# A decoder layer on one core: softmax on ScalarE, one memory region for the feed-forward block, and operand sums moved into the first unit

## The chip, the cores and the metric

The kernel runs on one core of a Trainium2 chip. The metric is the device time of one execution in microseconds (us). A core has five engines that run side by side, each with a queue of its own: TensorE (PE, whose weight loads are shown apart as PEld), VectorE (DVE), ScalarE (ACT), GpSimd (POOL) and SyncE (SP), whose queue issues the DMA transfers here. SBUF is the working memory, PSUM the memory that PE writes to.

## What is computed

One pre-norm decoder layer over x of shape (4, 2048, 512): a recurrence along the first axis (four steps), cross attention to a context of 77 keys for each of the four rows with 16 heads of 32, and a feed-forward block whose hidden size is 2048 and whose weights are a dense matrix times a butterfly, on the way up and on the way down. All of it is fp32. Cut to what matters:

```python
def _L0_xattn_ref(query, context, Wq, Wk, Wv, Wo):
    Q = (query @ Wq.T).reshape(B, T_q, N_HEADS, D_HEAD)
    K = (context @ Wk.T).reshape(B, T_c, N_HEADS, D_HEAD)
    V = (context @ Wv.T).reshape(B, T_c, N_HEADS, D_HEAD)
    scale = jnp.sqrt(jnp.asarray(D_HEAD, dtype=query.dtype))
    scores = jnp.einsum('bqhd,bkhd->bhqk', Q, K) / scale
    attn = jax.nn.softmax(scores, axis=-1)
    out = jnp.einsum('bhqk,bkhd->bqhd', attn, V).reshape(B, T_q, D)
    return out @ Wo.T

def _L0_ffn_ref(x, W_exp, b_exp, up_weights, up_bias, down_weights, W_con, b_con, down_bias):
    h = jnp.einsum('bsd,dh->bsh', x, W_exp) + b_exp
    h = butterfly(h, up_weights, D_HIDDEN)
    h = jax.nn.gelu(h + up_bias, approximate=False)
    h = butterfly(h, down_weights, D_HIDDEN)
    y = jnp.einsum('bsh,hd->bsd', h, W_con) + b_con
    return y + down_bias

x = x + _L0_attn_ref(_layernorm(x, axis=-1), ...)
x = x + _L0_xattn_ref(_layernorm(x, axis=-1), ctx_1024, ...)
x = x + _L0_ffn_ref(_layernorm(x, axis=-1), ...)
```

## The kernel before

**Preparation.** `_prepare` (L321) multiplies each butterfly into its dense matrix on the chip. The products pass through two large tiles: `wup` (4 x 2048 floats a partition) and `wdn` (16 x 512). At its end, the loop at L464 makes the 16 blocks of the down matrix with PE (L466) and evicts them into `wdn`. The down product isn't multiplied plainly, but by a scheme of 26 products of blocks, whose right operands are blocks of this matrix (`PLAIN`) and sums of them (`RIGHT`, 18 sums in two lots of nine). After every fourth block the sums of one quarter (j = 0 to 3) are made at once, half of them on DVE and half on POOL (L483, with one L480 among them), in a stretch of `wup` that is free by then, and stored in `dn26` in HBM (L484). The plain blocks are stored at the end (L488). Each sum has 256 elements a partition.

**Units.** The 2048 columns are worked in 16 units of 128. A unit has a front (`front`, L609: norm, recurrence, norm, query projection, attention, output projection, norm) and a feed-forward part (`feed_forward`, L738). The front of unit u + 1 is a generator, of which pieces are taken in between the feed-forward's matmuls of unit u (`step`, L750): PE has the work of both in its queue. The front of unit 0 runs inside the preparation, and the feed-forward of unit 15 has no front beside it. The projections and the up product run as seven block products for eight (`seven`, L593, and `up_head`, `up_mid`, `up_tail`), so operand sums on DVE and POOL stand ahead of them: `t2`, `t3` at L634 to L636, `sw` at L703 to L706, and `combine` (L727), which makes t1, t2 on DVE (L732, L734) and t3, n4 on POOL (L733, L735).

**Attention.** For each row t the four groups of four heads have one score matmul each (L662), into one of the two banks of PSUM tag "f", which all of the front shares. DVE takes the maximum of each head (L666) and subtracts it (L667), ACT makes the exponentials of the four heads in one instruction (L668). After four groups DVE sums (L670) and inverts (L671), and POOL multiplies (L672). After the scores of row t + 1 PE transposes the probabilities of row t (L684); the copies to SBUF alternate between DVE (L689) and ACT (L687), and the products with the values follow (L694).

**Output projection.** The first of the seven products goes to three quarters of xt. `spread` (L714) copies it from PSUM by ACT (L715) and adds it three times on POOL (L717); the other products are added to xt by DVE (L712).

**Feed-forward.** Eight steps p, each with weights of 896 KB (`w_up`, L779) and three PSUM tags a, b, c of two banks each; four Gelus a step on ACT (L772), and DVE's sums in between. Their outputs go into four `quarter` tiles. In the second half and through the down product POOL makes the left operands (L821, `made`) in the order of `_down_plan`. The down product is 26 products (L857), whose operands are loaded in turn into three weight buffers, and whose results DVE adds to xt (L872, L874). POOL adds the last bias to xt in eight pieces (L832).

**Memory.** The preparation's tiles lie in a pool (`prep`) that is closed after it. The feed-forward's pools (`xlast`, `acts`, `wts0` to `wts2`, `ffn`) are opened then and take over its memory, so that their first tiles wait for the last use of what lay there. `xlast` holds the x of every third unit.

**Order.** Inside the preparation PE, SP and POOL take their instructions in the order in which the program writes them; later the scheduler of the language orders each engine's queue, by the program's order and what it reckons to be ready. SP's queue holds all DMA issues in one line.

## Time and profile before

The median of three runs is 2778.08 us (2777.43 to 2786.68). The profiled execution took 2783.32 us, of which 2781.5 are the span from its first to its last instruction.

| group of instructions | count | busy us | mean ns |
|---|---|---|---|
| ACT exp, L668 (four heads, 308 elements) | 256 | 109.1 | 457 |
| ACT table loads, L668 and L772 | 75 + 75 | 192.4 | 1283 |
| ACT Gelu from SBUF, L772 | 384 | 194.8 | 508 |
| ACT Gelu from PSUM, L772 | 128 | 60.0 | 469 |
| DVE maximum, L666 | 256 | 119.9 | 473 |
| DVE subtraction, L667 | 256 | 113.8 | 470 |
| DVE sum, L670 (1232 elements) | 64 | 91.1 | 1424 |
| POOL multiplication, L672 (1232 elements) | 64 | 143.9 | 2248 |
| POOL addition in spread, L717 (512 elements) | 48 | 59.5 | 1269 |
| DVE addition of a projection, L712 (512 elements) | 96 | 66.0 | 687 |

Busy time is what the engine spent on instructions of the group; where neighbours overlap, the mean times the count is more than the busy time. In the lines of a timeline the columns are start, busy time, engine, line and operation, output and input, shape and count; in brackets stands how long the engine idled before and what ended that. In the lines of waits they are who waited, for whom, the sum in us, how often, and the longest.

### The profile page before, as it was taken

What the parts mean: (1) busy time and instruction counts of PE and PEld (TensorE: products, weight loads), DVE (VectorE), ACT (ScalarE), POOL (GpSimd) and SP (SyncE); (2) the same over time, 40 slices, a digit from 0 to 9 for tenths busy, and PEclk for the clock granted to TensorE, in tenths of its full rate; (3) what the DMA queues carried; (4) which work ended last, traced back from release to release, by engine and by line L of the source; (5) the groups of instructions that cost most, each with busy time, mean ns of one, the idle gap of its engine ahead of it and who ended that gap; (6) DMA issues with size and microseconds to landing.
All of it is one profiled execution on the core that took longest, in us unless ns stands there. A gap on an engine that the chain in (4) does not pass through costs nothing.

```text
span 2781.5 us, 37646 instructions
## 1 busy us (share of the span) xinstructions
PE 2564.9 (92%) x14280; PEld 2153.5 (77%) x14280; DVE 1610.1 (58%) x3653; ACT 840.9 (30%) x1484; POOL 1110.5 (40%) x957
## 2 busy tenths in 40 slices
PE   8886999898999989899998999999999998989999
PEld 5765778787878878787887878778787877878788
DVE  6666555555665655566555556655565565556542
ACT  2331414134241412424141341514234150422411
POOL 4543441626244261614416252351624335162434
PEclk9997999999999999999999999999999999999999
DMA  5736253443535344353534435253353534334356
GB/s 168 242 110 228 106 184 115 152 177 122 212 118 189 111 163 166 121 212 117 181 119 152 178 122 211 103 178 136 131 193 113 203 125 159 143 137 180 119 186 238
DMA packets 137894, 439.54 MB, mean 158 GB/s; under 512 B 20209, under 2 KB 46961, under 8 KB 134897
## 3 DMA queue, kind: packets, MB, share of 16 engines
q1 hardware_dynamic: 137714, 437.13, 43.9%
q8 instruction: 114, 1.87, 0.3%
q14 instruction: 66, 0.54, 0.1%
HBM read 398.27 MB, written 38.81 MB: 157 GB/s over the span
## 4 chain that ended last, share of the span: by engine, by line
PE 54%; DVE 19%; POOL 17%; DMA 4%; issue 3%; ACT 2%; SPq 1%; POOLq 0%; DVEq 0%; ACTq 0%
PE ps_b L767 9%; PE ps_c L767 6%; PE ps_q L604 6%; PE ps_a L767 5%; PE ps_w L604 4%; POOL pr L672 4%; POOL x L821 4%; POOL tb L821 4%; PE ps_b L857 4%; PE ps_s L619 3%; POOL q L821 3%; PE ps_pt L684 3%; DMA w_up<-up 3%; PE ps_sc L662 3%; DVE st L525 3%
## 5 line engine op out<-in xcount | busy, mean ns | idle before, releaser
L767 PE MATMUL ps_b<-tb,w_up 128*128 128x256 f32 x1512 | 392.0, 380 | 0.0
L672 POOL TENSOR_TENSOR pr<-pr,sm 128x1232 f32<-128x1232 f32 x64 | 143.9, 2248 | 440.1 <-DVE sm L671 436.7
L767 PEld LDWEIGHTS ps_b<-tb,w_up 128*128 128x128 f32 x1512 | 281.5, 190 | 39.9 <-issue 2.8
L772 ACT ACTIVATE q<-q,hbias 128x256 f32<-128x256 f32 x384 | 194.8, 508 | 334.7 <-DVE q L808 207.2
L767 PE MATMUL ps_a<-xnt,w_up 128*128 128x256 f32 x1008 | 262.8, 381 | 7.6 <-DMA w_up<-up 7.1
L561 ACT COPY xnt<-ps_t 128x512 f32<-128x512 f32 x128 | 73.7, 588 | 566.5 <-PE ps_t L560 566.5
L684 PE MATMUL ps_pt<-ident,pr 128*77 128x128 f32 x1024 | 166.1, 304 | 83.6 <-POOL pr L672 81.0
L821 POOL TENSOR_TENSOR x<-q 128x512 f32<-128x512 f32 x32 | 40.6, 1268 | 502.9 <-ACT q L772 502.9
L684 PEld LDWEIGHTS ps_pt<-ident,pr 128*77 128x77 f32 x1024 | 132.4, 164 | 130.4 <-POOL pr L672 98.5
L767 PEld LDWEIGHTS ps_a<-xnt,w_up 128*128 128x128 f32 x1008 | 188.0, 190 | 38.9 <-DMA w_up<-up 13.5
L712 DVE TENSOR_TENSOR xt<-ps_w,xt 128x512 f32<-128x512 f32 x96 | 66.0, 687 | 208.4 <-POOL xt L717 118.3
L689 DVE COPY pt<-ps_pt 77x512 f32<-77x512 f32 x128 | 87.5, 684 | 144.1 <-PE ps_pt L684 143.9
L662 PE MATMUL ps_sc<-kbd,qt 128*128 128x308 f32 x512 | 161.9, 427 | 7.4 <-DVE pr L667 6.7
L604 PE MATMUL ps_q<-xnt,wq 128*128 128x256 f32 x640 | 151.1, 379 | 0.0
L821 POOL TENSOR_TENSOR q<-q,x 128x512 f32<-128x512 f32 x48 | 61.1, 1273 | 225.1 <-PE ps_a L857 223.9
L604 PE MATMUL ps_w<-wo,sw 128*128 128x256 f32 x512 | 124.3, 386 | 28.1 <-DVE xt L712 23.9
L857 PE MATMUL ps_b<-w_dn,q 128*128 128x256 f32 x640 | 148.5, 379 | 0.0
L666 DVE TENSOR_REDUCE mx<-ps_sc 128x4 f32<-128x308 f32 x256 | 119.9, 473 | 42.2 <-PE ps_sc L662 37.0
L668 ACT ACTIVATE pr<-pr 128x308 f32<-128x308 f32 x256 | 109.1, 457 | 108.1 <-DVE pr L667 106.6
L687 ACT COPY pt<-ps_pt 77x512 f32<-77x512 f32 x128 | 74.2, 580 | 215.9 <-PE ps_pt L684 215.7
L821 POOL TENSOR_TENSOR x<-q,q 128x512 f32<-128x512 f32 x80 | 114.2, 1428 | 61.9 <-ACT q L772 55.6
L857 PE MATMUL ps_b<-w_dn,x 128*128 128x256 f32 x512 | 135.9, 384 | 0.0
(236 smaller groups left out, 5616.4 us busy)
## 6 DMA issues: line engine op xcount, KB each, us to landing
w_dn<-dn SPq DMA_DIRECT2D x416, 512.0 KB, 4.2
w_up<-up SPq DMA_DIRECT2D x126, 896.0 KB, 4.5
wq<-wq SPq DMA_DIRECT2D x16, 1792.0 KB, 8.4
xt<-in_x SPq DMA_DIRECT2D x16, 1024.0 KB, 5.4
out<-xt SPq DMA_DIRECT2D x48, 256.0 KB, 2.4
dn<-wup SPq DMA_DIRECT2D x8, 1152.0 KB, 5.2
wdn<-in_wexp_t SPq DMA_DIRECT2D x4, 1024.0 KB, 10.3
wdn<-in_wcon SPq DMA_DIRECT2D x4, 1024.0 KB, 4.8
```

Of the source, the lines that this page charges most:

```text
L525: keep(nc.vector.bn_stats(st[:, t, :], xt[:, t, :]))
L604: nc.tensor.matmul(tiles[key][:, r, :], lhsT=lhs(i, r, k), rhs=rhs(i, r, k), start=key == i and r == 0 and k == 0, stop=k == 1, skip_group ...
L662: nc.tensor.matmul(ps[:, 0 : 4 * NK], lhsT=qt[:, g, t, :], rhs=kbd[:, t, g, :], start=True, stop=True)
L666: nc.vector.tensor_reduce(mx, sc, AX.X, ALU.max)
L668: nc.scalar.activation(pg, pg, AF.Exp, scale=1.0 / math.sqrt(DH))
L672: nc.gpsimd.tensor_tensor(pr, pr, sm.unsqueeze(2).to_broadcast([P, NH, NK]), ALU.mult)
L684: nc.tensor.transpose(pt_ps[0:NK, j, :], pr[:, 4 * g + j, :], ident)
L689: nc.vector.tensor_copy(pt, pt_ps[0:NK])
L767: nc.tensor.matmul(ps, lhsT=w[:, c, :], rhs=rhs[i - 1][:, c], start=first and c == 0, stop=c == 1, skip_group_check=True)
L772: nc.scalar.activation(out, x, AF.Gelu, bias=hbias[:, b : b + 1])
L821: nc.gpsimd.tensor_tensor(place(p), place(x), place(y), ALU.add if op == "+" else ALU.subtract)
L857: nc.tensor.matmul(ps, lhsT=left[:, j, :], rhs=pair[:, n, j, :], start=first and j == 0, stop=j == NB // 4 - 1, skip_group_check=True)
```

## The change

It has four parts.

- **Softmax.** The keys are scaled by -1/sqrt(32) when they are laid out, so that a score comes out negated. DVE takes the minimum of each head; ACT makes the exponential of each head by itself, straight from PSUM, with the minimum as bias and a scale of -1, and delivers the sum with it (`accum_out`). The subtraction and the sum on DVE go. DVE instead of POOL multiplies by the inverse.
- **Spread.** DVE adds the first product of the output projection to three quarters of xt straight from PSUM; ACT's copy and POOL's additions go.
- **One region.** `arena` is one tile of 20480 floats a partition that lives through the whole kernel. The preparation's `wup`, `wdn` and `low` and, after it, xlast, the sums' places, tb, p1, u2, u3, two of the three weight buffers and the four quarters are slices of it. The weights of the up product's third and fourth step are loaded ahead of the first unit.
- **Operand sums.** Those of quarter 0 are made in the preparation, on POOL alone; those of quarters 1 to 3 in the first three steps of unit 0, seven on DVE and eleven on POOL each. The blocks of `wdn` are laid in the order in which they are made, and all eight plain blocks of a quarter are stored with its sums. A sign is turned in e and in the right operand 4. In unit 0 the last bias is added in two pieces.

```diff
-FIRST = 0, NB // 2, NB // 4, 3 * NB // 4
+ORDER = [k + j for j in range(4) for k in (0, NB // 2, NB // 4, 3 * NB // 4)]
...
-PLAIN = ("b01", "b10", "b11", "b20", "b30", "b31")
+PLAIN = tuple(f"b{k}{n}" for k in range(4) for n in range(2))
+SLOW = "12", "9", "7", "18", "15", "16", "20", "17", "10", "19", "22"
...
+def _right_sums(nc, j, wdn, rings, dn26, alone):
+
+    made = {f"b{k}{d}": wdn[:, 4 * j + k, d * (D // 2) : (d + 1) * (D // 2)] for k in range(4) for d in range(2)}
+    for lot, ring in zip(RIGHT, rings):
+        w = ring.rearrange("p (s d) -> p s d", s=len(lot))
+        for i, (name, x, op, y) in enumerate(lot):
+            made[name] = w[:, i, :]
+            x, y, op = made[x], made[y], ALU.add if op == "+" else ALU.subtract
+            if alone or name in SLOW:
+                nc.gpsimd.tensor_tensor(made[name], x, y, op)
+            else:
+                nc.vector.tensor_tensor(made[name], x, y, op)
+        first = SLOT[lot[0][0]]
+        nc.sync.dma_start(out=dn26[first : first + len(lot), :, j, :].rearrange("s p d -> p s d"), in_=w)
+    nc.sync.dma_start(out=dn26[2 * len(RIGHT[0]) : 2 * len(RIGHT[0]) + 8, :, j, :].rearrange("s p d -> p s d"),
+                      in_=wdn[:, 4 * j : 4 * j + 4, :].rearrange("p k (n d) -> p (k n) d", n=2))
...
-            nc.vector.tensor_copy(kbd[q, :, g, j * NK : (j + 1) * NK],
-                                  ps[q, 0 : T * NK].rearrange("p (b k) -> p b k", b=T))
+            nc.vector.tensor_scalar(kbd[q, :, g, j * NK : (j + 1) * NK], ps[q, 0 : T * NK].rearrange("p (b k) -> p b k", b=T),
+                                    -1.0 / math.sqrt(DH), None, ALU.mult)
...
+    arena = const.tile([P, 80 * P * 2], F32, name="arena")
...
                 pr = work.tile([P, NH, NK], F32, tag="pr", name="pr")
+                sm = small.tile([P, NH], F32, tag="sm", name="sm")
...
-                    nc.vector.tensor_reduce(mx, sc, AX.X, ALU.max)
-                    nc.vector.tensor_tensor(pg, sc, mx.unsqueeze(2).to_broadcast([P, 4, NK]), ALU.subtract)
-                    nc.scalar.activation(pg, pg, AF.Exp, scale=1.0 / math.sqrt(DH))
-                sm = small.tile([P, NH], F32, tag="sm", name="sm")
-                nc.vector.tensor_reduce(sm, pr, AX.X, ALU.add)
+                    low = small.tile([P, 4], F32, tag="low", bufs=4, name="low")
+                    nc.vector.tensor_reduce(low, sc, AX.X, ALU.min)
+                    for h in range(4):
+                        nc.scalar.activation(pr[:, 4 * g + h, :], sc[:, h, :], AF.Exp, bias=low[:, h : h + 1], scale=-1.0,
+                                             accum_out=sm[:, 4 * g + h : 4 * g + h + 1])
                 nc.vector.reciprocal(sm, sm)
-                nc.gpsimd.tensor_tensor(pr, pr, sm.unsqueeze(2).to_broadcast([P, NH, NK]), ALU.mult)
+                nc.vector.tensor_tensor(pr, pr, sm.unsqueeze(2).to_broadcast([P, NH, NK]), ALU.mult)
...
         def spread(ps):
-            nc.scalar.copy(w1, ps)
             for r in (r12, r22, r21):
-                nc.gpsimd.tensor_tensor(r, r, w1, ALU.add)
+                nc.vector.tensor_tensor(r, ps, r, ALU.add)
...
+            if u == 0 and p < 3:
+                _right_sums(nc, p + 1, wdn, rings, dn26, False)
...
+            if u:
+                nc.gpsimd.tensor_tensor(r, r, ybias[:, d], ALU.add)
+            elif p % 2 and p > h // 2:
+                r = xt[:, p - 5 : p - 3, :]
+                nc.gpsimd.tensor_tensor(r, r, ybias.unsqueeze(1).to_broadcast([P, 2, D]), ALU.add)
...
+    sizes = [("xlast", T * D)] + [(n, D) for n in own] + [("tb", 4 * D)] + [(f"{n}{i}", 2 * P) for i in range(2) for n in ("p1", "u2", "u3")]
+    sizes += [("w1", 4 * D), ("w2", 4 * D)] + [(f"q{k}", 4 * D) for k in (2, 3, 0, 1)]
...
+    rings = [arena[:, i * 9 * D // 2 : (i + 1) * 9 * D // 2] for i in range(2)]
...
-        wup = pool.tile([P, NC, HID], F32, name="wup")
-        wdn = pool.tile([P, NB, D], F32, name="wdn")
+        wup = arena[:, 0 : NC * HID].rearrange("p (c n) -> p c n", c=NC)
+        wdn = arena[:, NC * HID : NC * HID + NB * D].rearrange("p (b d) -> p b d", b=NB)
+        low = arena[:, NC * HID + NB * D : NC * HID + NB * D + NB * 2 * (P - 1)]
...
+            if n == 27:
+                _right_sums(nc, 0, wdn, rings, dn26, True)
...
+    wts = [pool.tile([P, 4 * D], F32, tag="w", name="w"), homes["w1"], homes["w2"]]
...
+    early += [up_weights(2), up_weights(3)]
```

## The prediction

> **What bounds the kernel now.** I read the head of the page first, then the stretches of time, then the waits of the steady part, then the timeline of the two places where waits are long.
>
> ```profile
> span 2781.5 us, 37646 instructions
> PE 2564.9 (92%) x14280; PEld 2153.5 (77%) x14280; DVE 1610.1 (58%) x3653; ACT 840.9 (30%) x1484; POOL 1110.5 (40%) x957
> ```
>
> TensorE (PE) is busy 92% of the span, the next engine 58%. The change leaves the matmuls as they are, so it can only win from the 216.6 us in which PE idles, and from matmuls that run slowly after an idle stretch. Where are these 216.6 us? In the table by stretches the columns are length, then busy time of PE, PEld, DVE, ACT, POOL, then PE's clock.
>
> ```profile
> 176.00:203.00 27.00, 20.12 (x71) 11.15 (x70) 19.76 (x52) 10.70 (x19) 13.54 (x16) 0.87 0.44 145
> 203.00:250.00 47.00, 21.18 (x71) 16.61 (x70) 29.61 (x59) 5.80 (x12) 23.54 (x28) 0.70 0.84 274
> 727.00:888.00 161.00, 151.04 (x851) 127.20 (x851) 95.31 (x216) 50.64 (x89) 63.81 (x50) 1.00 0.43 156
> ```
>
> The passage from the weight preparation to the first unit (176 to 250 us) idles 32.7 of 74 us, at a clock down to 0.70. A steady unit idles some 10 of 162. So there are two things to price. First the steady waits, over thirteen units (560 to 2660 us):
>
> ```profile
> PE ps_pt L684 <- POOL pr L672: 72.0, 39, 2.8
> PE ps_t L560 <- DVE xn L551: 27.1, 25, 1.1
> PE ps_w L604 <- DVE xt L712: 22.2, 13, 1.7
> ```
>
> PE waits for the normalised probabilities from POOL 5.5 us a unit (72.0/13), and 1.7 (22.2/13) at the output projection, where DVE's L712 is itself held by POOL's L717 (DVE idles 118.3 us there over the run). Second, the passage:
>
> ```profile
> 189.64 1.11 PE L560 MATMUL ps_t<-ident,xn 128*128 128x128 f32 x4 [6.88 <-DVE xn L551]
> 220.86 2.07 PE L767 MATMUL ps_b<-tb,w_first 128*128 128x256 f32 x4 [15.85 <-DVE tb L734]
> 234.91 2.08 PE L767 MATMUL ps_c<-xnt,w_first 128*128 128x256 f32 x4 [5.74 <-DVE q L800]
> 246.63 1.09 PE L589 MATMUL ps_t<-ident,xp 128*128 128x128 f32 x4 [4.15 <-DVE xp L578]
> 188.29 0.42 DVE L483 TENSOR_TENSOR wup<-wdn,wup 128x256 f32<-128x256 f32 x1 [3.58 <-POOL wup L483]
> 234.43 0.42 DVE L800 TENSOR_TENSOR q<-ps_c,u 128x256 f32<-128x256 f32 x1 [7.38 <-DMA dn<-wdn]
> ```
>
> The operand sums (L483) keep DVE and POOL until 219 us, so t1 and t2 (L732, L734) come late; then the quarter buffers, carved out of the preparation's released memory, wait for its last stores (L488).
>
> **What the Trainium skill says.** (1) "ScalarE: Activation LUTs", What ACT_TABLE_LOAD costs: an ACTIVATE costs about 280 ns + 0.833 ns an element with a pointer as bias, 186 ns with immediates; neighbours overlap by 93; a change of table is a 1283 ns load. The trace agrees: biased Gelu of 256 elements 508 ns from SBUF and 467 from PSUM, unbiased exp of 308 457 ns, loads 1283. No section read prices the accumulator output. (2) "SBUF — State Buffer", Who interferes with whom: a DVE instruction with two SBUF inputs contends with a GpSimd instruction reading SBUF, one with a single SBUF input doesn't. The trace agrees: L635 (512 elements) takes 692 ns at best and 1736 in the median beside POOL's L634; L483 0.41 and 0.94. (3) "TensorE: Matmul & The Clock Gate", What's actually happening: after an idle window of about 3.4 us TensorE runs at half clock until it has been busy for as long. The trace agrees: after the 15.85 us gap four matmuls take 1.87 us from start to start, 0.86 when warm.
>
> **The change part by part.** The sum is against the profiled execution, 2783.3 us (span 2781.5 and 1.8 around it), which stands 5.2 above the median 2778.1.
>
> *Operand sums (L473 to L488).* Removed from the preparation: 72 sums, 36 on each engine, and the gaps 6.88 + 15.85 + 5.74 + 4.15 = 32.6 us. Slow matmuls after the gaps cost, from start to start in PE's timeline against the warm rate (1.87 against 0.86 for the first four at 220.86), 2.3 + 2.1 + 1.9 + 2.1 = 8.4 behind the four gaps. Together 41.0 is the most to be had. Added: quarter 0, eighteen sums on POOL alone, from about 183 us (where POOL's first L483 starts) at 0.72 to 0.97, so 13 to 17.5, until about 198. Its three stores stand in SP's queue ahead of the second early weight load (L955), the bias load (L469) and the ybias loads: w_second, issued at 191.5 before, goes out at about 200 and lands 4.5 later (the page's w_up row). Meanwhile PE, without the 6.88, ends the preparation near 197 and reaches w_second five groups (4.3 us) later: a new wait of about 3.5 us, and 2 of slow clock. POOL's t3 (L733) follows at 198 to 199.5, just in time. First xn still waits about 1. Quarters 1 to 3 run under unit 0's first three steps: 7 sums on DVE (0.41 to 0.94) and 11 on POOL (0.85) each, 20 and 28 us in all, beside front 1, whose norm (L578) PE waited for already: I leave 4 of the 4.15 and 2 more. Sum kept: 1 + 3.5 + 2 + 6 = 12.5, gain 28. Bounds: 38 if nothing new shows, 10 if the stores in SP's queue also delay the weights of steps 2 to 4. The 24 unsummed pieces grow to 32 stores' worth in fewer DMAs: nothing, they land 70 us before use.
>
> *One region.* The wait at L800 is counted above; later allocations in it cost nothing, as only `w_up` loads show (6.7/13 = 0.5 us a unit). ybias in unit 0, two large adds for eight: POOL idles there, nothing.
>
> *spread (L714 to L717).* ACT loses 16 x 0.59, POOL 48 x 1.27 = 59.5; DVE gains 48 x 0.69 = 33 us against 118.3 in which it stood. The PSUM tile is held 2.1 instead of 0.6 us, hidden by the eight matmuls of product 6 (1.7) and the feed-forward's between. What is late next is the L712s in their own order. Gain 1.7 a unit.
>
> *Softmax (L664 to L672).* DVE loses the subtraction (256 x 0.470 = 120 at one by one) and the sum (64 x 1.42), POOL 64 x 2.25 = 144. The multiplication on DVE isn't in the trace: L483's 0.41 at 256 and L635's 0.69 at 512 elements give 1.46 us at 1232, the contended pair (0.94, 1.74) 4.0. I take 1.5 at the first row, where POOL idles, and 2.5 to 4 after; behind it on DVE queue the copies of pt (L689) and the additions of down products (L872), whose PSUM tags are two banks deep, so that PE has one product (some 0.9 us) of cover: this is part of the 3 us charged below. ACT: four activations of 77 elements with a pointer bias from PSUM for one of 308. From Gelu's 467 by 0.85 an element (copies: 370 at 256, 588 at 512) one is 315; neighbours overlap by 77 (two exps take 0.84). So at least 238 each (accumulator free), at most 315 (no overlap); I take 262, 1.05 a group and 4.2 a row, where it was 1.65. ACT rises by 64 x 2.55 = 163 us, which is no bound in itself (36% of the span).
>
> The chain of one row, from the last exp: before 1.42 + 0.24 + 2.25 = 3.9 us and POOL's queue; after 0.24 + 1.5 to 4.0. The exps themselves end 2.5 later. First row: about equal, better by 1. Third and fourth row, where ACT is idle and POOL full of feed-forward sums: exps end at about 819 and 825.5 of the unit 727 to 888, product at 823 and 829.5, against the 823.97 and 831.6 at which PE came to wait. So 1.8 + 2.8 us of wait go. Against it stands ACT in the two first rows:
>
> ```profile
> 798.75 1.28 ACT L772 ACT_TABLE_LOAD   x1
> 800.05 0.51 ACT L772 ACTIVATE q<-q,hbias 128x256 f32<-128x256 f32 x1
> 800.57 1.28 ACT L668 ACT_TABLE_LOAD   x1
> 801.87 0.84 ACT L668 ACTIVATE pr<-pr 128x308 f32<-128x308 f32 x2
> 802.73 1.28 ACT L772 ACT_TABLE_LOAD   x1
> ```
>
> From 791.4 to 805 Gelu and exp alternate, with six table loads, and ACT doesn't rest. Eight groups grow by 0.63 each: 5.1 us later (4.3 to 6.8), and behind them queue the last Gelus, on which POOL's sums and so the down products wait, and the copies of pt (L687), which hold the two banks of the transposes. PE's order lets other matmuls in; I charge 3 us a unit of 5.1, bounds 0 and 9. POOL starts its sums later, but has 4.5 us of multiplications less between them.
>
> Steady: 5.5 + 1.7 - 3 = 4.2 us a unit, fifteen times (fronts 1 to 15), 63. Total 28 + 63 = 91: 2692, in medians 2687; rounded 2688.
>
> **Rivals.**
> - A, as above: 2688, its own range 2660 to 2728. 0.60.
> - B, ACT's lateness is hidden by PE's reordering: 38 + 15 x 7.2 = 146 gone, 2632. For it: only 0.88 us of wait at the first row today. Against: ACT is full there. 0.12.
> - C, the wait for POOL becomes one for ACT and DVE of the same size: only the passage wins, 2750, or 2768 at its lower bound. For it: two PSUM banks for scores, now held by four exps. 0.13.
> - D, slower: ACT decides in the mixed stretch. Six heads' more openings let Gelu and exp alternate more: 6.8 us of exps and two more pairs of loads (5.1), 11.9 a unit. It decides from 7.2 + 28/15 = 9.1 us on; at 11.9 the run is 15 x 4.7 - 28 = 43 longer, 2821. Against: ACT idles from 788 to 791 and after 818. 0.12.
> - E, the change doesn't do what it says: waits within the single region count unrelated parts as one, and each of eight weight loads a unit shows its 4.5 us: 36 a unit, over 3300. The accesses are plain separate ranges. 0.03.
>
> **How the numbers follow.** A measurement tells 0.5% (14 us) from nothing. Faster: A, B and half of C, 0.79; within 0.5%: the other half of C, 0.06; slower: D and E, 0.15. The range runs from the middle of B (2640) to C (2755), leaving out about 0.2.
>
> **What would show it.** Right: L684 no longer waits for pr by more than 1 us; no wait of PE above 5 us between 180 and 250, and the first unit's third step about 28 us earlier; unit period 158. Wrong: PE waiting at L684, L662 or the down products for ACT by more than 9 us a unit, over 75 pairs of table loads, exps above 315 ns, or a wait of w_up longer than 5 us in unit 0.

## The result, and the profile after

The changed kernel takes 2766.24 us (median of 9 runs, 2757.82 to 2775.01) against 2778.17 (9 runs, 2773.90 to 2786.68): a ratio of 0.9953, 95% interval 0.9934 to 0.9972. It is faster by half a percent, where 2688 us was forecast. The profiled execution (2760.3 us) lies at the lower end of its runs, and that of before 5 us above its median, so the two profiled executions differ by 23.0 us where the medians differ by 11.9. Below, profiles explain the places and medians the sizes.

Head of the page, after:

```profile
span 2758.6 us, 39105 instructions
PE 2563.0 (93%) x14280; PEld 2144.6 (78%) x14280; DVE 1560.5 (57%) x3426; ACT 1053.9 (38%) x3262; POOL 948.2 (34%) x858
```

POOL lost 162 us, and ACT gained 213, with 1778 instructions more. PE is as busy as it was. The three stretches that the prediction showed of before, in the same table (length; busy time of PE, PEld, DVE, ACT, POOL; PE's clock):

```profile
176.00:203.00 27.00, 26.23 (x123) 17.46 (x122) 17.24 (x38) 12.74 (x23) 11.81 (x15) 1.00 0.13 44
203.00:250.00 47.00, 34.32 (x148) 27.54 (x147) 34.70 (x72) 10.98 (x23) 32.86 (x39) 0.89 0.81 269
727.00:888.00 161.00, 151.13 (x846) 127.08 (x845) 91.76 (x202) 63.69 (x200) 53.03 (x43) 0.99 0.46 154
```

The passage has filled: PE's idle time in it fell from 32.7 to 13.5 us, and the clock there rose. The steady unit hasn't: PE is busy 151.1 of 161 us, as before, though POOL has 10.8 us less to do in it and ACT 13 more. The waits of PE over thirteen steady units (560 to 2660 us; total, times, longest) show what became of the two waits that the change was to end:

```profile
PE ps_a L859 <- POOL arena L817: 46.8, 13, 3.6
PE ps_t L560 <- DVE xn L551: 27.2, 25, 1.2
PE ps_w L604 <- DVE sw L703: 21.6, 13, 1.7
PE ps_c L859 <- ACT arena L769: 14.6, 13, 1.1
PE ps_a L764 <- DMA arena<-up: 7.5, 12, 1.2
PE ps_q L604 <- DVE tq L636: 5.1, 13, 0.4
PE ps_o L693 <- DVE pt L688: 4.1, 4, 1.0
```

The wait for POOL's probabilities (72.0 us before) is gone. In its place PE waits at the down products, 3.6 us a unit for POOL's operands and 1.1 for a Gelu. The wait of 1.7 at the output projection has the same size and another cause: it was for DVE's addition at L712, and is now for the operand sum sw (L703), which waits for s1 (L702) on POOL. Now the chain that leads to the 3.6 us, in one unit of the timeline (start, duration):

```profile
780.90 1.28 ACT L668 ACT_TABLE_LOAD   x1
782.20 0.33 ACT L668 ACTIVATE pr<-ps_sc,low 128x77 f32<-128x77 f32 x1
782.42 0.19 ACT L668 ACTIVATION_READ_ACCUMULATOR pr<-ps_sc,low 128x1 f32 x1
782.51 0.32 ACT L668 ACTIVATE pr<-ps_sc,low 128x77 f32<-128x77 f32 x1
...
784.78 1.28 ACT L769 ACT_TABLE_LOAD   x1
...
805.54 30.41 POOL L817 TENSOR_TENSOR arena<-arena 128x512 f32<-128x512 f32 x22 [39.34 <-ACT arena L769]
...
804.64 0.70 PE L859 MATMUL ps_c<-arena 128*128 128x256 f32 x2 [1.12 <-ACT arena L769]
807.92 1.46 PE L859 MATMUL ps_a<-arena 128*128 128x256 f32 x6
812.98 2.93 PE L859 MATMUL ps_a<-w,arena 128*128 128x256 f32 x6 [3.60 <-POOL arena L817]
```

The same place on POOL before, where t1 stands at 722.52:

```profile
809.46 1.27 POOL L821 TENSOR_TENSOR tb<-q,q 128x512 f32<-128x512 f32 x1
814.65 1.27 POOL L821 TENSOR_TENSOR x<-q,q 128x512 f32<-128x512 f32 x1 [3.91 <-ACT q L772]
```

The sum that an exponential gives out is an instruction of its own, so that a head takes two, and heads follow each other by 0.30 us (782.20, 782.51): 1.2 us a group. From 781 to 806 us ACT alternates between Gelus, exponentials, one copy or another and table loads, and idles for 0.16 us in all. POOL's 22 sums for the down product wait for Gelus at the end of this stretch and start 93.4 us after the unit's t1 (712.10 on DVE). Before, one sum ran 86.9 us after t1 and the others waited for the last Gelu until 92.1 after it. Against before, the row of sums is thus only 1.3 us later; but PE, whose order is another, stands ready for an operand of theirs from 809.4 us on, 97.3 after t1. It waits 3.60 us, and then does six matmuls in 2.93 us that took 1.46 just ahead of the gap: half the pace, and the clock that the trace records for 812 to 816 us is 0.57.

In the passage PE has more waits than before, but short ones:

```profile
207.72 1.56 PE L764 MATMUL ps_b<-arena,w_first 128*128 128x256 f32 x4 [3.36 <-DVE arena L360]
216.74 1.13 PE L764 MATMUL ps_a<-xnt,w_second 128*128 128x256 f32 x4 [2.70 <-DMA w_second<-up]
226.58 2.07 PE L764 MATMUL ps_a<-xnt,w 128*128 128x256 f32 x4 [3.54 <-DMA w<-up]
233.81 0.63 PE L589 MATMUL ps_t<-ident,xp 128*128 128x128 f32 x4 [1.75 <-DVE xp L578]
254.30 1.13 PE L764 MATMUL ps_b<-arena 128*128 128x256 f32 x4 [2.94 <-DVE arena L795]
...
204.08 2.98 DVE L141 TENSOR_TENSOR arena<-arena 128x256 f32<-128x256 f32 x3 [4.32 <-DMA dn<-arena]
206.98 0.68 DVE L360 COPY arena<-ps_p 128x512 f32<-128x512 f32 x1
```

The first of them has a cause that is easy to overlook. DVE's sums of quarter 1 (L141) write into the ring from which quarter 0 is still being stored, so they wait 4.32 us for that store; the eviction of a last block (L360) stands behind them on DVE and holds PE at 207.72.

And one loss lies ahead of the passage, in the front of unit 0, where PE takes its instructions in the program's order (the first two lines are of after, the third, in a fence of its own, of before):

```profile
134.82 0.79 PE L663 MATMUL ps_sc<-kbd,qt 128*128 128x308 f32 x2 [1.56 <-ACT pr L668]
136.74 4.41 PE L467 MATMUL ps_p<-bd,arena 128*128 128x128 f32 x24
```

```profile
132.51 2.84 PE L450 MATMUL ps_p<-bd,wdn 128*128 128x128 f32 x24
```

The scores of the next group wait for a bank that the exponentials hold, and the 24 matmuls behind take 4.41 us instead of 2.84. By the start of the down matrix's blocks PE is 8.5 us late (178.30 before, 186.84 after). With the exponentials of before in the kernel after (e1, below) that start is at 180.07, so most of the delay is theirs.

### The profile page after: what moved, and what is told of

Same layout as the page of the kernel before. It is cut to its first block, busy times and chain, and to the rows that moved or that the text cites. A ratio compares the mean times of both kernels' runs of the same rounds, so it can differ in the third digit from the quotient of the medians.

```text
span 2758.6 us, 39105 instructions
## 1 busy us (share of the span) xinstructions
PE 2563.0 (93%) x14280; PEld 2144.6 (78%) x14280; DVE 1560.5 (57%) x3426; ACT 1053.9 (38%) x3262; POOL 948.2 (34%) x858
## 4 chain that ended last, share of the span: by engine, by line
PE 65%; DVE 14%; ACT 9%; POOL 5%; DMA 4%; issue 2%; SPq 0%; DVEq 0%; POOLq 0%; ACTq 0%
PE ps_b L764 9%; PE ps_b L859 7%; PE ps_c L764 6%; PE ps_q L604 6%; PE ps_w L604 5%; PE ps_a L764 5%; PE ps_a L859 5%; PE ps_c L859 5%; PE ps_sc L663 4%; POOL arena L817 3%; DMA arena<-up 3%; ACT pr L668 3%; PE ps_s L619 3%; PE ps_pt L683 3%; DVE st L525 3%; ACT L769 2%
## 5 line engine op out<-in xcount | busy, mean ns | idle before, releaser
L817 POOL TENSOR_TENSOR arena<-arena 128x512 f32<-128x512 f32 x448 | 606.6, 1373 | 1385.5 <-ACT arena L769 1092.1
L668 ACT ACTIVATE pr<-ps_sc,low 128x77 f32<-128x77 f32 x1024 | 317.5, 332 | 145.7 <-DVE low L666 143.7
L769 ACT ACTIVATE arena<-arena,hbias 128x256 f32<-128x256 f32 x384 | 192.0, 508 | 318.2 <-DVE arena L804 189.7
L764 PE MATMUL ps_b<-arena 128*128 128x256 f32 x1128 | 290.1, 379 | 2.9 <-DVE arena L795 2.9
L764 PEld LDWEIGHTS ps_b<-arena 128*128 128x128 f32 x1128 | 211.1, 190 | 34.9 <-DVE arena L795 3.3
L668 ACT ACTIVATION_READ_ACCUMULATOR pr<-ps_sc,low 128x1 f32 x1024 | 216.4, 211 | 0.0
L859 PE MATMUL ps_b<-arena 128*128 128x256 f32 x896 | 214.3, 379 | 0.0
L764 PE MATMUL ps_a<-xnt,arena 128*128 128x256 f32 x752 | 196.4, 384 | 9.1 <-DMA arena<-up 9.1
L859 PE MATMUL ps_a<-w,arena 128*128 128x256 f32 x512 | 148.4, 417 | 50.4 <-POOL arena L817 50.4
L663 PE MATMUL ps_sc<-kbd,qt 128*128 128x308 f32 x512 | 185.2, 450 | 9.0 <-ACT pr L668 6.7
L859 PEld LDWEIGHTS ps_b<-arena 128*128 128x128 f32 x896 | 165.6, 190 | 22.8
L859 PE MATMUL ps_c<-arena 128*128 128x256 f32 x640 | 164.7, 381 | 15.7 <-ACT arena L769 15.7
L764 PEld LDWEIGHTS ps_a<-xnt,arena 128*128 128x128 f32 x752 | 141.6, 191 | 34.6 <-DMA arena<-up 15.1
```

The source lines that it names most:

```text
L663: nc.tensor.matmul(ps[:, 0 : 4 * NK], lhsT=qt[:, g, t, :], rhs=kbd[:, t, g, :], start=True, stop=True)
L668: nc.scalar.activation(pr[:, 4 * g + h, :], sc[:, h, :], AF.Exp, bias=low[:, h : h + 1], scale=-1.0, accum_out=sm[:, 4 * g + h : 4 * g + h ...
L764: nc.tensor.matmul(ps, lhsT=w[:, c, :], rhs=rhs[i - 1][:, c], start=first and c == 0, stop=c == 1, skip_group_check=True)
L769: nc.scalar.activation(out, x, AF.Gelu, bias=hbias[:, b : b + 1])
L817: nc.gpsimd.tensor_tensor(place(p), place(x), place(y), ALU.add if op == "+" else ALU.subtract)
L859: nc.tensor.matmul(ps, lhsT=left[:, j, :], rhs=pair[:, n, j, :], start=first and j == 0, stop=j == NB // 4 - 1, skip_group_check=True)
```

## The experiments

All times are medians; before took 2778 to 2781 us beside them. The scheduler orders each variant anew, so a variant differs from its neighbour by more than its edit; that is why several edits were tried from more than one side. The table gives, from one profiled execution each, the start of the first t1 in `combine` (it ends the preparation), the length of unit 0 (t1 to t1) and the mean length of units 1 to 14, all in us. Between one set of runs and another the median of before itself moved by 3 us, so differences between rows of that size say little. "Exps" tells the form: one exponential of 308 a group with a subtraction on DVE, four of 77 with the sum on DVE, or four with their own sums.

| kernel | exps | s1 on | us | ratio, 95% | first t1 | unit 0 | unit |
|---|---|---|---|---|---|---|---|
| before | one | POOL | 2778.2 | | 219.4 | 179.3 | 162.7 |
| after | four, own sums | POOL | 2766.2 | 0.9953 (0.9934 to 0.9972) | 197.3 | 191.7 | 161.8 |
| e1_old_exp | one | POOL | 2733.6 | 0.9839 (0.9820 to 0.9858) | 190.6 | 189.3 | 160.5 |
| e2_no_accum | four | POOL | 2691.7 | 0.9687 (0.9669 to 0.9704) | 192.1 | 193.9 | 157.3 |
| e3_softmax_alone | four, own sums | POOL | 2778.8 | 1.0003 (0.9989 to 1.0017) | 226.8 | 175.0 | 162.0 |
| e4_idle_exps | one, three idle | POOL | 2889.9 | 1.0399 (1.0378 to 1.0419) | | | |
| e5_pool_mult | four | POOL | 2875.8 | 1.0352 (1.0334 to 1.0369) | | | |
| e6_sums_in_prep | four | POOL | 2706.4 | 0.9743 (0.9728 to 0.9758) | 195.8 | 204.9 | 157.4 |
| e7_early_loads | four | POOL | 2695.6 | 0.9701 (0.9687 to 0.9716) | | | |
| e8_s1_on_dve | one | DVE | 2622.4 | 0.9440 (0.9425 to 0.9456) | 192.0 | 185.2 | 152.8 |
| e9_after_s1 | four, own sums | DVE | 2752.4 | 0.9894 (0.9876 to 0.9912) | 197.8 | 193.9 | 161.3 |
| e10_no_accum_s1 | four | DVE | 2678.5 | 0.9631 (0.9617 to 0.9646) | 194.8 | 191.3 | 156.2 |
| e11_old_spread | one | DVE | 2637.1 | 0.9483 (0.9468 to 0.9497) | 195.4 | 185.5 | 153.5 |
| e12_before_three_moves | one | DVE | 2639.5 | 0.9492 (0.9477 to 0.9507) | 224.3 | 169.5 | 152.9 |

**The exponentials of before in the kernel after.** The multiplication stays on DVE.

```diff
-                    for h in range(4):
-                        nc.scalar.activation(pr[:, 4 * g + h, :], sc[:, h, :], AF.Exp, bias=low[:, h : h + 1], scale=-1.0,
-                                             accum_out=sm[:, 4 * g + h : 4 * g + h + 1])
+                    pg = pr[:, 4 * g : 4 * g + 4, :]
+                    nc.vector.tensor_tensor(pg, sc, low.unsqueeze(2).to_broadcast([P, 4, NK]), ALU.subtract)
+                    nc.scalar.activation(pg, pg, AF.Exp, scale=-1.0)
+                nc.vector.tensor_reduce(sm, pr, AX.X, ALU.add)
```

> The changed kernel with the exponentials of before: DVE subtracts the minimum, ACT makes four heads in one instruction, DVE sums; the multiplication stays on DVE. ACT theory (the longer exponentials delay the last Gelus, so POOL's sums start late and PE waits at the down product): the wait of PE for POOL's L818 falls below 0.5 us a unit from 3.6, front 0 gets its 8 us back, 2690 us (2675 to 2710), ratio to before 0.968. Rival 1 (DVE's multiplication and spread delay what POOL waits for): the wait stays at 3 to 4 us a unit, 2755 to 2775. Rival 2 (POOL's chain of 22 sums is the bound by itself, whenever it starts): the same, 2755 to 2775.

2733.6 us, outside both expected ranges. The wait at the down product is gone, and another has come forward (waits of PE, 560 to 2660 us, then the timeline):

```profile
PE ps_w L604 <- DVE sw L704: 68.9, 13, 5.3
```

```profile
814.65 1.89 PE L604 MATMUL ps_w<-wo,ot 128*128 128x256 f32 x8
...
823.56 3.75 PE L604 MATMUL ps_w<-wo,sw 128*128 128x256 f32 x8 [5.30 <-DVE sw L704]
```

Without the late exponentials PE arrives early at the output projection, and s1 (here L703) stands on POOL behind the sums of the feed-forward (it starts at 820.39, the moment after the 21st of them). This second queue is about as large as the first; it was hidden behind it.

**Four exponentials without their sums.**

```diff
-                        nc.scalar.activation(pr[:, 4 * g + h, :], sc[:, h, :], AF.Exp, bias=low[:, h : h + 1], scale=-1.0,
-                                             accum_out=sm[:, 4 * g + h : 4 * g + h + 1])
+                        nc.scalar.activation(pr[:, 4 * g + h, :], sc[:, h, :], AF.Exp, bias=low[:, h : h + 1], scale=-1.0)
+                nc.vector.tensor_reduce(sm, pr, AX.X, ALU.add)
```

> The changed kernel with four exponentials a group but no accumulator output; DVE sums as before. It takes 1024 reads of the accumulator off ACT, some 95 us of pace (0.30 to 0.21 us a head), and puts 64 x 1.42 = 91 us on DVE. ACT theory: half of the delay goes, the wait of PE for POOL falls from 3.6 to 1 to 2 us a unit, 2725 (2705 to 2750). Rivals: unchanged or slower by the longer chain of a row, 2760 to 2790.

2691.7 us, 75 below after and below the expected range. ACT in the groups of lines (count, then busy us and mean ns), first of after, then of this kernel, and one burst of eight in this kernel's timeline:

```profile
L668 ACT ACTIVATE pr<-ps_sc,low 128x77 f32<-128x77 f32 x1024 | 317.5, 332 | 145.7 <-DVE low L666 143.7
L668 ACT ACTIVATION_READ_ACCUMULATOR pr<-ps_sc,low 128x1 f32 x1024 | 216.4, 211 | 0.0
```

```profile
L668 ACT ACTIVATE pr<-ps_sc,low 128x77 f32<-128x77 f32 x1024 | 238.1, 336 | 90.8 <-DVE low L666 89.9
```

```profile
781.08 1.84 ACT L668 ACTIVATE pr<-ps_sc,low 128x77 f32<-128x77 f32 x8
```

The mean of one is the same (332 and 336 ns), the pace isn't: eight in 1.84 us are (1.84 - 0.34)/7 = 0.21 us each, against 0.30 with the sums. The wait for POOL at the down product falls from 3.6 to 0.7 us a unit (9.3 in thirteen). DVE makes 64 sums of 1232 elements more, and PE's wait for its probabilities is 0.3 us a unit (3.7 in thirteen). That this kernel beats e1 by 42 us, with slower exponentials, is not explained by its edit: PE has another order in it and waits 1.7 us a unit for sw instead of 5.3. Over twelve units PE idles 5.9 us a unit in it and 8.6 in e1, which is most of the difference; what made the order so wasn't traced. With s1 out of the way (below) the order of the two is the expected one.

**The softmax alone, in the kernel before.** The minimum and its negative scale, the four exponentials with their sums and the multiplication on DVE; memory, spread and operand sums as before.

```diff
-                    nc.vector.tensor_tensor(pg, sc, mx.unsqueeze(2).to_broadcast([P, 4, NK]), ALU.subtract)
-                    nc.scalar.activation(pg, pg, AF.Exp, scale=1.0 / math.sqrt(DH))
...
+                        nc.scalar.activation(pr[:, 4 * g + h, :], sc[:, h, :], AF.Exp, bias=low[:, h : h + 1], scale=-1.0,
+                                             accum_out=sm[:, 4 * g + h : 4 * g + h + 1])
...
-                nc.gpsimd.tensor_tensor(pr, pr, sm.unsqueeze(2).to_broadcast([P, NH, NK]), ALU.mult)
+                nc.vector.tensor_tensor(pr, pr, sm.unsqueeze(2).to_broadcast([P, NH, NK]), ALU.mult)
```

> The kernel before with the new softmax alone (keys scaled, minimum, four exponentials with sums, multiplication on DVE). ACT theory: PE's wait for pr on POOL (5.5 us a unit) goes and a wait for POOL's L821 of about 3.5 us with slow clock after it comes, front 0 loses 8 us: 2785 (2770 to 2800), same or slower than before. If the softmax is a gain that other parts of the change spoil: 2700 to 2740.

2778.8 us over 14 runs: nothing, to 0.2%. Its waits are those of after (46.8 us for POOL at L820, 21.6 for sw). So the softmax part as a whole is worth zero when it is added to before, and from there to after the rest of the change gives the 12 us of the result. Its first t1 stands 7.4 us later than before's (226.8 and 219.4), the loss in the front of unit 0, of which unit 0 gives 4.3 back (175.0 for 179.3).

**Three idle exponentials a group on top of e1**, into the spent score bank; their values are used by nothing.

```diff
                     nc.scalar.activation(pg, pg, AF.Exp, scale=-1.0)
+                    for h in range(3):
+                        nc.scalar.activation(sc[:, h, :], sc[:, h, :], AF.Exp, bias=low[:, h : h + 1], scale=-1.0)
```

> e1 with three idle exponentials of 77 elements behind each group, written into the score bank that is no longer needed: ACT's load and the holding of the bank come back, DVE's part and all data stay as in e1. They pace at some 0.2 to 0.25 us each, 0.65 to 0.75 a group, where the changed kernel has 0.8 more than e1. ACT theory: the wait for POOL's sums comes back at 3 us a unit or more, 2750 to 2785. Rivals: within 10 us of e1. The idle exponentials are work that the result doesn't need.

2889.9 us, 156 above e1 and far above the expected range. The groups of ACT:

```profile
L671 ACT ACTIVATE ps_sc<-ps_sc,low 128x77 f32<-128x77 f32 x768 | 216.4, 295 | 9.5
...
L772 ACT ACT_TABLE_LOAD x120 | 154.0, 1283 | 50.1 <-PE ps_a L767 34.8 <-DVE hbias L486 13.3
L671 ACT ACT_TABLE_LOAD x104 | 133.4, 1283 | 1.9
...
L669 ACT ACT_TABLE_LOAD x16 | 20.5, 1283 | 0.3
```

The table loads rose from 152 to 240, so the run had two doses at once: 768 exponentials and 88 x 1.28 = 113 us of loads. It doesn't price an exponential. It does show that time added to ACT reaches PE, at 39% of the span (PE's wait for a score bank held by ACT is only 2.1 us in the thirteen units, its waits for POOL's sums 59.8), and that more openings for exponentials can make the two functions alternate more, the mechanism of rival D; in the change itself the loads stayed at 76 pairs (75 before).

**The multiplication back on POOL, in e2.**

```diff
-                nc.vector.tensor_tensor(pr, pr, sm.unsqueeze(2).to_broadcast([P, NH, NK]), ALU.mult)
+                nc.gpsimd.tensor_tensor(pr, pr, sm.unsqueeze(2).to_broadcast([P, NH, NK]), ALU.mult)
```

> e2 (2692 us) with the multiplication of the probabilities back on POOL. Prediction's theory: PE's wait for pr comes back at 3.5 to 5.5 us a unit, and POOL's sums in the second half of the unit are held 4.5 us more: 2755 (2735 to 2780). Rival: e2's order of work covers it, within 10 us of e2.

2875.8 us, 184 above e2, far more than expected. Waits of PE, 560 to 2660 us:

```profile
PE ps_pt L683 <- POOL pr L671: 99.1, 24, 7.7
...
PE ps_a L859 <- POOL arena L817: 26.5, 12, 2.2
```

The move off POOL was the right one here, and worth more than the wait of 5.5 us that before shows for it: with later exponentials the multiplications land deeper in POOL's stretch of feed-forward sums, and both waits come.

**All operand sums in the preparation, in e2.**

```diff
-            if u == 0 and p < 3:
-                _right_sums(nc, p + 1, wdn, rings, dn26, False)
...
-            if n == 27:
-                _right_sums(nc, 0, wdn, rings, dn26, True)
+            if n in (27, 31, 35, 39):
+                _right_sums(nc, (n - 27) // 4, wdn, rings, dn26, False)
```

> e2 with all operand sums in the preparation, after each fourth block, on DVE and POOL as in the first unit; the region stays. If the move of the sums is worth what the first combine shows (22 us), 2712; if unit 0 pays it back (its time from combine to combine rose by 12 to 14 us), the first combine is 15 to 20 later, unit 0 12 to 15 shorter and the run 2698 (2690 to 2706).

2706.4 us, 14.7 above e2. The first t1 is only 3.7 us later (195.8), where 15 to 20 were expected: with the region as it is, sums in the preparation no longer hold it for long. And unit 0, which was to be shorter, is longer (204.9 against 193.9 us), above all by one wait of PE (180 to 420 us):

```profile
PE ps_a L764 <- DMA w<-up: 30.2, 1, 30.2
```

In SP's queue the stores of all four quarters (the last issued at 229.6 to 234.2) stand ahead of the load of the third step's weights, which goes out at 237.2. The run thus prices this order of SP's queue as much as the place of the sums.

**Bias and second weights loaded ahead of quarter 0's stores, in e2.**

```diff
-        if n == NB // 2:
+        if n == 2:
...
-            if n == 28:
+            if n == 26:
```

> e2 with the load of w_second and of the bias b1 issued ahead of the stores of quarter 0 in SP's queue. If these stores hold the loads up, PE's waits for w_second (2.7 us) and w (3.5) and the slow clock after them go: 2684 (2680 to 2688). If another wait takes their place (the sums on DVE and POOL): 2690 to 2694.

2695.6 us, against 2691.7 for e2: no gain. PE no longer waits for w_second, and waits 8.6 us for DVE's norm (xp, L578) and up to 4.1 for xn (L551) instead, where e2 has 2.8 and 2.0. The load wasn't the last thing to arrive in this passage; why the norm comes later wasn't traced.

**s1 of the output projection on DVE, in e1.**

```diff
-        nc.gpsimd.tensor_tensor(s1, a21, a22, ALU.add)
+        nc.vector.tensor_tensor(s1, a21, a22, ALU.add)
```

> e1 (2734 us) with the first operand sum of the output projection, s1, on DVE instead of POOL. In e1 it stands behind the feed-forward's sums in POOL's queue, and PE waits 5.3 us a unit for s2 and then runs eight matmuls at half clock (1.9 us). If this order on POOL is e1's cost: that wait falls below 1 us, 15 x 5 to 7 us gone, 2640 (2625 to 2665). If the next sum (s4) takes its place: 2700 to 2735.

2622.4 us, ratio 0.944 (0.9425 to 0.9456): the fastest kernel of the study, a little below the expected range. All that PE waits for in thirteen units (and the page's head):

```profile
PE ps_t L560 <- DVE xn L551: 27.0, 25, 1.1
PE ps_a L765 <- DMA arena<-up: 6.1, 9, 1.4
PE ps_q L604 <- DVE tq L636: 5.0, 13, 0.4
```

```profile
PE 2525.8 (96%) x14280; PEld 2135.7 (81%) x14280; DVE 1728.6 (66%) x3762; ACT 831.8 (32%) x1470; POOL 934.5 (36%) x842
```

Both queues are gone: 152.8 us a unit. DVE is 168 us busier than after, and it costs nothing.

**The same edit in after.** One line, as above. The two theories part here: if ACT's late exponentials are what holds the unit, s1 gives little; if POOL's queue is, it gives what it gave in e1.

> The changed kernel with s1 of the output projection on DVE. If ACT's longer exponentials are the cause of the wait for POOL's L817 (3.6 us a unit) and for the Gelu (1.1), these stay and only the wait for sw (1.7) goes: 2738 (2720 to 2755). If POOL's order around s1 is the cause of both, as it was of e1's: 2640 (2620 to 2665).

2752.4 us, 14 below after: with s1 out of the way, the late exponentials by themselves hold the unit at 161.3 us. The wait for sw falls to 0.5 us a unit, and the wait at the down product is what it was:

```profile
PE ps_a L859 <- POOL arena L817: 46.8, 13, 3.6
...
PE ps_c L859 <- ACT arena L769: 14.6, 13, 1.1
```

**And in e2.** The same line.

> e2 (four exponentials a group without accumulator) with s1 on DVE: the middle dose of ACT's work between e8 (one exponential a group, 2622 us) and e9 (four with accumulator). ACT theory: only e2's wait for sw goes, 1.7 us a unit: 2662 (2650 to 2675), between the two others. Rival (accumulator reads cost by something of their own, not by ACT's time): it comes within 8 us of e8.

2678.5 us, somewhat above the expected range. With s1 on DVE in all three the forms of the exponentials stand in a row: one 2622, four 2678, four with their own sums 2752. Splitting costs 56 us and the sums 74, where all else is equal (the order apart). The start of POOL's sums for the down product, counted from the unit's t1 in the same unit of each timeline, follows: 86.6 us (e8), 90.1 (e10), 93.8 (e9). With s1 on POOL it is 86.7 (e1), 89.8 (e2), 93.4 (after).

**The spread of before, in e8.**

```diff
+            nc.scalar.copy(w1, ps)
             for r in (r12, r22, r21):
-                nc.vector.tensor_tensor(r, ps, r, ALU.add)
+                nc.gpsimd.tensor_tensor(r, r, w1, ALU.add)
```

> e8 (2622 us) with the spread of before: ACT copies the first product, POOL adds it three times. By the prediction's working the change of spread is worth 1.7 us a unit, 25 in all: 2647. If the next sum in line made PE wait anyway, as sw did in the changed kernel, and e8 has no such wait left: 2622 to 2630.

2637.1 us, 14.7 above e8, between the two expected outcomes: the spread on DVE is worth 0.7 us of each steady unit (153.5 and 152.8), where 1.7 was forecast, and 3.4 us ahead of the first.

**Three moves to DVE in the kernel before.** Its exponentials, memory and operand sums stay.

```diff
-                nc.gpsimd.tensor_tensor(pr, pr, sm.unsqueeze(2).to_broadcast([P, NH, NK]), ALU.mult)
+                nc.vector.tensor_tensor(pr, pr, sm.unsqueeze(2).to_broadcast([P, NH, NK]), ALU.mult)
...
-        nc.gpsimd.tensor_tensor(s1, a21, a22, ALU.add)
+        nc.vector.tensor_tensor(s1, a21, a22, ALU.add)
...
-            nc.scalar.copy(w1, ps)
...
-                nc.gpsimd.tensor_tensor(r, r, w1, ALU.add)
+                nc.vector.tensor_tensor(r, ps, r, ALU.add)
```

> The kernel before with its own exponentials, memory and operand sums in the preparation, and three pieces of work moved from POOL to DVE: the multiplication of the probabilities, the spread, and s1. If the steady part's gain comes from POOL's relief alone and not from the region or the moved sums: e8 plus what the passage is worth, 2622 + 20 to 30 = 2648 (2640 to 2658). If the region is needed for it: 2680 to 2740.

2639.5 us, ratio 0.9492 (0.9477 to 0.9507). The unit takes 152.9 us, the same as e8: all of the steady gain is the relief of POOL, and none of it needs the new exponentials or the one region. What the region and the moved sums give is 17.1 us. The table shows how: the first t1 comes 32.3 us earlier in e8 (192.0 for 224.3), and unit 0 gives 15.6 back (185.2 for 169.5, from unrounded times). How the steady gain divides between the multiplication and s1 wasn't tried in this kernel.

## Why the prediction was wrong, step by step

**The steady unit** was to gain 5.5 + 1.7 - 3 = 4.2 us and gained 0.9 (162.7 to 161.8). The runs lead from before to after by two ways, in us a unit:

| part | forecast | by e12, e8 and e9 | by e1 |
|---|---|---|---|
| multiplication and spread off POOL | -7.2 | -9.8, with s1 (before to e12) | -2.2, without s1 (before to e1) |
| region, sums of unit 0 | 0 | -0.1 (e12 to e8) | in the line above |
| form of the exponentials | +3 | +8.5 (e8 to e9) | +1.3 (e1 to after) |
| s1 left on POOL | not named | +0.5 (e9 to after) | in the first line |
| sum | -4.2 | -0.9 | -0.9 |

The ways differ because two things hold the unit, and either is enough: with s1 on POOL alone it takes 160.5 us (e1), with the late exponentials alone 161.3 (e9), with both 161.8, with neither 152.8 (e8). So two steps of the prediction failed, and each by itself would have left a gain of only 1.4 to 2.2 us a unit.

The first is the charge for ACT's lateness: "PE's order lets other matmuls in; I charge 3 us a unit of 5.1, bounds 0 and 9". With nothing else in the way it is 8.5, inside the bounds, at the end that was named and not taken. The delay itself was nearly right. Eight groups were to grow by 0.63 each, 5.1 us; they grew by 1.2 - 0.42 = 0.78, which makes 6.2, and POOL's sums start 6.7 us later in after than in e1 (93.4 and 86.7). What was wrong was the discount: PE paid more than the delay. Over twelve units PE idles 9.0 us a unit in e9 and 3.2 in e8, and its matmuls take 152.6 us instead of 149.9. In e8 the recorded clock stays full in these units; in e9 it falls to one half in most of them, for 3.4 or 6.8 us behind the wait of 3.6.

The second is the account of what is late next when the spread's wait is gone, "the L712s in their own order". It was s1 on POOL. With the late exponentials away this is 160.5 - 152.8 = 7.7 us a unit, 111 us in all (e1 to e8); in after it is 14 (e9), because the second queue shows only when the first is gone.

The 7.2 for the two freed waits was sound as far as it went, given that s1 moves too: from before to e12 PE's idle time falls by 7.1 us a unit (10.3 to 3.2). What it left out is that the matmuls then take 149.9 us instead of 152.7: the prediction charged slow matmuls behind gaps in the passage and not in the unit.

**The price of the exponentials** entered that charge. Taken were 262 ns, with 238 for a free accumulator and 315 without overlap. Without the sums a head takes 0.21 us, below the lower bound; the sum adds an instruction, recorded at 211 ns, which lengthens the pace by 0.09, to 0.30, inside the bounds but above what was taken. That the range held this pace is in part luck: the activation was cheaper than its lower bound, and the sum wasn't free. ACT rose by 213 us instead of 163. One sign of error was badly chosen: "exps above 315 ns" is met by e2 as well (336 ns), because records of neighbours overlap. Here only the distance of starts gave the pace.

**The passage** was to gain 28 us. By e3 and after, which share the softmax and differ in the rest of the change (the spread among it), the first t1 comes 29.5 us earlier (226.8 to 197.3), and unit 0 is 16.7 longer (175.0 to 191.7): 12.8 kept. On the fast base (e12 to e8) 17.1 is kept. That the removed sums had held the passage is borne out; the sum of new losses, 12.5, was too small. (The 72 sums removed are 40 on DVE and 32 on POOL by the trace of before, not 36 each.) The w_second wait was foreseen at 3.5 and came at 2.70. The third step's weights (3.54) were named only in the lower bound, a gain of 10, and not foreseen were DVE's wait for the ring's store with the eviction behind it (3.36) and the sum at L795 (2.94). All quarters in the preparation are worse by 14.7 (e6), but with the third step's weights behind their stores; whether moving the sums is needed with those weights loaded first wasn't tried.

**The front of unit 0** wasn't priced at all. There PE is in the program's order, and the new exponentials hold the score banks; the first t1 of e3 comes 7.4 us later, and 3.1 are left after unit 0. The prediction spoke of reordering by PE, which doesn't hold inside the preparation.

**The DVE multiplication** was priced at 1.5 us at the first row and 2.5 to 4 after. Its 64 instructions average 1.57 us: the 34 beside an idle POOL took 1.44, the 30 beside POOL's sums 1.72 in the mean. The contention is there, and POOL pays most of it: beside each of these 30 one of POOL's sums took 2.46 us in the mean, where the median is 1.27 and none took over 1.73 before. That is some 2.4 us a unit (30 x 1.19 / 15) of POOL's time, which the forecast doesn't have. In min, median and max, in ns:

```profile
L671 DVE TENSOR_TENSOR pr<-pr,sm x64: 1422/1443/2543, 119.5 to 2615.8; 128x1232 f32<-128x1232 f32 x64
L817 POOL TENSOR_TENSOR arena<-arena x448: 1252/1267/2554, 257.8 to 2743.4; 128x512 f32<-128x512 f32 x150
```

DVE carried 168 us more still (e8) without holding PE.

**The rivals.** C, in which the wait for POOL comes back in the same size and the passage alone wins, gave 2750, or 2768 at its lower bound, which is nearest to the result. In its make-up it is only half right: the wait came back at the down product and not at the transposes, and the passage isn't all that won. In the profiles the first t1 and unit 0 together gain 9.7 us (22.1 less 12.4) and the fourteen units after them 12.7, so the nearness of the number is in part luck. D, ACT deciding, was to turn the sign from 9.1 us a unit; at 8.5 it came close. E didn't happen: PE's wait for weights is 0.6 us a unit (7.5 in thirteen), and 0.5 before. The direction was right, but by the prediction's own limit of 14 us the 11.9 us lie among the outcomes "within 0.5%", which it gave 0.06. Two of its signs of being right came true (no wait for pr at the transposes, none above 5 us between 180 and 250) while the gain did not: they named the old waits, and PE waited elsewhere.

## What to carry to other kernels

An engine that is 38% busy over the span can be full for 25 us of every unit; here time added to it there came back in full, and the slow matmuls behind the new wait with it. A discount for work that fills the gap should name that work from the timeline. When work is taken off a queue, look for everything else in that queue that PE waits for: here one addition of 1.27 us, moved to the engine with room, decided between 1.6% and 5.6% once the exponentials were short. The losses of two such queues don't add: either one alone kept most of the gain away. Ask of each part of a combined change whether it is needed for the gain: moving the multiplication, the spread and one addition to DVE gives 5.1% by itself, and with the region and those moves in place the new form of the exponentials cost 130 us (e8 to e9).

## What the runs showed of the hardware

- **The sum of an activation is a second instruction.** ACTIVATION_READ_ACCUMULATOR follows each of the 1024 exponentials and slows their pace from 0.21 to 0.30 us. The Trainium skill, "VectorE: DVE Perf Modes", Two Vector instructions with no wait between them, says of VectorE that an operation which writes out its accumulator is two instructions, the main one and a read; the trace shows the same on ScalarE.
- **Short gaps cost clock too.** The Trainium skill, "TensorE: Matmul & The Clock Gate", What's actually happening, puts the fall of the clock behind an idle window of about 3.4 us. Here the slow matmuls come after a gap of 3.60 us, as it says, but also after gaps of 1.56 and 0.44 us in the front of unit 0 (4.41 us for 24 matmuls, 2.84 before, there behind a gap of 1.05). In before's units from 996 us on it fell to one half once in each, behind waits of 1.8 and 2.8 us with 6 us between them, though in the two units ahead of these the same waits left it full; in the units of e2, e8, e10, e11 and e12, where PE's longest wait is 1.7 us or less, the recorded clock is full from 560 to 2500 us.
- **DVE's multiplication and POOL's sums hold each other up, and either can pay.** The Trainium skill, "SBUF — State Buffer", Who interferes with whom, which the prediction drew on, says that a DVE instruction with two SBUF inputs contends with a GpSimd instruction that reads SBUF. The trace agrees. In the unit shown, the multiplication at 830.92 takes 1.44 us, as if alone, but the sum that POOL starts at 831.10 takes 2.39 instead of 1.27; at 820.29 both are slowed (1.75 and 2.48). For L635 it is DVE that pays: 1.61 us in the mean, 0.69 at best.
